# Recurrence of a bidirectional WKV kernel: when the result rows are turned on TensorE, and in which order its last two tiles are summed

## The chip, the cores and the metric

The kernel runs on one core of a Trainium2 chip. The metric is the device time of one execution in microseconds (us), and the median of the runs is compared. Before the change three runs took 1113.6, 1116.46 and 1119.26 us, so the median is 1116.46. A profile of one further execution (1116.4 us) shows where the time goes. A core has five engines that each work through their own instructions in order and wait for one another by semaphores: TensorE (PE, with its weight loads PEld), VectorE (DVE), ScalarE (ACT), GpSimd (POOL) and SyncE (SP), which here only starts transfers. All numbers are float32.

## The reference

Two stages are computed on `x` of shape 4 x 1024 x 1024. The first is a recurrence over time in both directions; its result is the input of the second, two blocks of attention over 16 slots. Cut to what matters:

```python
ek = exp(min(k, 30));  ekv = ek * v              # here k = v = fside, r = x
a_t = a_{t-1} * decay + ekv_t                    # forward; the same in reverse
b_t = b_{t-1} * decay + ek_t
num = nf + nb - ekv + exp(min(u + k, 30)) * v
den = df + db - ek  + exp(min(u + k, 30))
x1  = sigmoid(r) * num / max(den, 1e-8) * (0.8 + 0.2 * tf)
for _ in range(2):                               # slot attention
    logits = rms(x1) @ compete_w.T + compete_b   # 16 slots; the 4 best tokens of each
    ...                                          # write slots, attend to them
    x1 = rms(x1 + x_b)
out = x + x1
```

## The kernel before

The recurrence works on 32 tiles `i` of 128 channels x 1024 time steps (4 batches, 8 tiles of channels each), with time along the free dimension. All work is issued in an order written out by hand (`pin`); each engine runs its own part of it in that order, so an instruction that waits holds up everything behind it on its engine. Of tile `i`, in the loop from L525:

- DVE makes four scans of 1024 steps (L314): forward over `ek`, forward over `ekv`, reverse over each (`den`, `num`), and three other passes (L354, L358, and L413 for tile `i - 1`). The reverse scans start from an edge value that ACT makes (L326) once the forward scan has ended.
- ACT computes the exponentials (L286, L306), the logarithm and exponential that make a reciprocal of `den` (L391, L393, `quo`), the square of the result (L428), and copies out of PSUM.
- POOL multiplies and clamps (L296, L302, L375, L406, L407) and makes the product of tile `i - 1` (L425), which is the result and also the last reader of that tile's `both` buffer. There are two such buffers.
- PE sums the numerators into `num` (L364), contracts the result (`gate`) and its square (in `quo`, of which there are two buffers) into `raw` for the logits (L436), and transposes the result into rows (`turn_half`, L450). These go through one PSUM bank, `ptr`, which a copy on ACT (L451) empties into `stage` before the next transposes; then ACT's queue sends `stage` to the rows in DRAM (L459). The same bank serves `projection`, 25 pieces of work on later weights (L481 to L506) that are strewn over the tiles.

Every fourth tile (`i % HK == 0`, HK is 4) ACT also computes the sigmoid of the next four tiles of `x` at once: a table load, one instruction over 128 x 4096, and a table load back (L273, L171). It stands between the two edges, in the place called `between`. `x` is loaded in groups of four tiles (`load_gates`), of which three are held. The rows of tile `i - 2` are turned in tile `i`, half by half, each half followed by its contraction of the square.

After the loop, from L592, the last tile is finished by halves: numerators, the rest of `raw`, then norms and logits of 1024 tokens x 16 slots x 4 batches. The transposes of tile 30's rows stand ahead of the last numerators, those of tile 31's rows after the logits. In `write_slots` the four best tokens of each slot are found and gathered from the rows in DRAM (L746); the gather waits until the last rows have landed.

Of the kernel before, what the change touches and what calls it, by code (L numbers as in the profile page):

```python
# [10 lines left out]
F32 = mybir.dt.float32  # L11
# [4 lines left out]
PSUM = bass.MemoryType.PSUM  # L16
DRAM = bass.MemoryType.DRAM

P = 128
# [19 lines left out]
def kernel(  # L39
# [71 lines left out]

    rc_stack = ExitStack()
    rc = rc_stack.enter_context(tc.tile_pool(name="rec_const", bufs=1))
    cond_sb = rc.tile([P, B, TD], F32, name="cond_sb")
# [3 lines left out]
    rec_stack = ExitStack()  # L118
    rec = rec_stack.enter_context(tc.tile_pool(name="rec", bufs=1))
    rec_ps = rec_stack.enter_context(tc.tile_pool(name="rec_ps", bufs=1, space=PSUM))  # L120

    def load(i):
        kf = rec.tile([P, L], F32, tag="kf", bufs=4, name=f"kf_{i}")
# [129 lines left out]
    with rec_stack:  # L253
# [176 lines left out]
        def contract(i, src, w, halves=(0, 1)):  # L430

            b, k = i // NK, i % NK
            rows_b = slice(32 * b, 32 * b + 32)
            for h in halves:
                pin(
                    nc.tensor.matmul(  # L436
                        raw[rows_b, ts(h, 512)],
                        lhs[:, w].rearrange("p h s -> p (h s)"),
                        src[:, ts(h, 512)],
                        start=(k == 0 and w == k),  # L440
                        stop=(k == NK - 1 and w == NK),
                    )
                )

        def turn_half(i, stage, h):

            xk = gate_of(i)
            ptr = rec_ps.tile([P, 4, P], F32, tag="ptr", bufs=1, name=f"ptr_{i}_{h}")
            for q in range(4):
                pin(nc.tensor.transpose(ptr[:, q, :], xk[:, ts(4 * h + q, P)], ident))  # L450
            pin(nc.scalar.copy(stage[:, 4 * h : 4 * h + 4, :], ptr))  # L451

        def staged(i):
            return rec.tile([P, NT, P], F32, tag="stage", bufs=1, name=f"stage_{i}")
# [67 lines left out]
        ek[0] = terms_exp(0, kf[0], halves)  # L522
        ek[1] = terms_exp(1, kf[1])
        ekv[0] = terms(0, kf[0], ek[0], halves)
        for i in range(N):  # L525
# [4 lines left out]
            both[i], edge[i] = sums_a(  # L530
                i,
                ek[i],
                ekv[i],
                [every] if past else halves,
                lambda: own_exp(i, kf[i], own[i]),
                lambda: gates(i // HK) if i % HK == 0 else None,
            )
            if i == 0:
                move(npost_col, npost.rearrange("(k p) -> p k", p=P))
                move(bo_col, bo.rearrange("(k p) -> p k", p=P))  # L540
            if i == 3:
                move(npost_bc, npost.partition_broadcast(P))
            if i % HK == 2 and i // HK + 2 < N // HK:
                load_gates(i // HK + 2)
            if 5 <= i < 9:
                wo_next.append(load_rows(wo, i - 5, f"wp{i - 5}"))
            if N // 2 - 2 <= i < N // 2 + 8 and i % 2 == 0:
                load_ahead(0, (i - N // 2 + 2) // 2)
            if i >= N - 2:
                for n in range(2):  # L550
                    load_ahead(0, 5 + 2 * (i - N + 2) + n)
            if older:
                stage = staged(i - 2)
                for h in range(2):
                    turn_half(i - 2, stage, h)
                    contract(i - 2, quo[i - 2], NK, (h,))
                send(i - 2, stage)
            for _ in range(min((0, 1, 2, 2)[i % HK], len(projection)) if i > HK * 2 else 0):
                projection.pop(0)()
            if past:  # L560
                gated(i - 1, both[i - 1], quo[i - 1])
            if i == HK:
                pin(
                    nc.gpsimd.tensor_tensor(
                        cw_next, cw_sb, npost_col.unsqueeze(2).to_broadcast([P, NK, S]), ALU.mult
                    )
                )
            if i + 1 < N:
                ekv[i + 1] = terms(i + 1, kf[i + 1], ek[i + 1])
            den_sum(both[i], own[i])  # L570
            floor(both[i])
            if past:
                newton(i - 1, both[i - 1], quo[i - 1], num_ps[i - 1])
                product(i - 1, both[i - 1][:, 0, :], nc.gpsimd)
                store_turned(i - 1)
            ov = own_value(i, kf[i], own[i])
            num_ps[i] = rec_ps.tile([P, L], F32, tag="num", bufs=1, name=f"num_{i}")
            add_negated(num_ps[i], ov, True)
            if i == N - 1:
                break  # L580
            numerator(i, both[i], edge[i])
            quo[i] = guess(i, both[i])
            if i + 2 < N:
                ek[i + 2] = terms_exp(i + 2, kf[i + 2])
            if past:
                square(i - 1, quo[i - 1])
# [11 lines left out]
        spread_cols = spread.rearrange("p b h s -> p (b h s)")  # L598
        quo[i] = guess(i, both[i], [part for _, part in halves])
        square(i - 1, quo[i - 1])  # L600
        stage = staged(i - 1)
        for h in range(2):
            turn_half(i - 1, stage, h)
        send(i - 1, stage)
        for h, part in halves:
            numerator_half(i, both[i], edge[i], h)
            gated(i, both[i], quo[i], part)
            add_negated(num_ps[i], both[i][:, 1, :], False, (h,))
        for h, part in halves:
            newton(i, both[i], quo[i], num_ps[i], part, num_ps[i])  # L610
            product(i, num_ps[i], nc.vector, part)
            square(i, quo[i], part)

        def spread_squares(h, part):
            pin(nc.vector.tensor_copy(raw_sb[:, part], raw[:, part]))
            pin(nc.tensor.matmul(sq[:, part], spread_cols, raw_sb[:, part], start=True, stop=True))

        for h, part in halves:
            contract(i - 1, gate_of(i - 1), NK - 2, (h,))
            if h == 0:  # L620
                spread_squares(*halves[0])
            contract(i - 1, quo[i - 1], NK, (h,))
            contract(i, gate_of(i), NK - 1, (h,))
            contract(i, quo[i], NK, (h,))
# [30 lines left out]
        norm_root(halves[1][1])  # L655
        norm_logits(halves[1][1])

        turned_last = rec_ps.tile([P, NT, P], F32, tag="num", bufs=1, name="turned_last")
        for t in range(NT):
            pin(nc.tensor.transpose(turned_last[:, t, :], gate_of(i)[:, ts(t, P)], ident))  # L660
        stage = rec.tile([P, 2, L], F32, tag="both", bufs=2, name="stage_last")[:, 0, :]
        stage = stage.rearrange("p (t c) -> p t c", c=P)
        for h in range(2):
            part = slice(4 * h, 4 * h + 4)
            pin(nc.scalar.copy(stage[:, part, :], turned_last[:, part, :]))
        send(i, stage)
    rc_stack.close()
    keep = ctx.enter_context(tc.tile_pool(name="keep", bufs=1))

# [651 lines left out]
```

## Time and profile before

| | us |
|---|---|
| median of three runs | 1116.46 (1113.6 to 1119.26) |
| the profiled execution | 1116.4 |
| its span, first to last instruction | 1114.6 |
| recurrence: last forward scan's tile starts | 410.49 |
| logits complete | 443.0 |
| the gather starts | 447.80 |
| attention, two blocks | the rest |

In the profile a line gives an instruction group as line, engine, operation and `out<-in`; a number with x is a count, and what stands in brackets is the time that the engine had been idle and what ended it. Each tile's start is taken where DVE's scan over `ek` starts. The granted clock is what TensorE was given: 1.00 is full speed, 0.50 half.

### The profile page before, as it was taken

The numbers are of one execution on the slowest core, as the hardware profiler recorded it, in microseconds if no ns is written. First come the engines' busy times: TensorE is split into PE (matmuls) and PEld (weight loads), VectorE is DVE, ScalarE is ACT, GpSimd is POOL, SyncE is SP. The second block draws the span as 40 slices with busy tenths as digits, with TensorE's granted clock in tenths as the row PEclk, the third lists the DMA queues.
The fourth block names the chain that finished last, engine by engine and source line by source line (L and its number), as shares of the span: only waits on it lengthen the run. The fifth ranks groups of instructions, "written<-read, shape, count | busy, mean of one in ns | idle before, by whom it ended". The sixth has DMA issues, their size and how long they took to land.

```text
span 1114.6 us, 11896 instructions
## 1 busy us (share of the span) xinstructions
PE 965.5 (87%) x4116; PEld 541.4 (49%) x4116; DVE 768.0 (69%) x1049; ACT 508.4 (46%) x791; POOL 546.4 (49%) x417
## 2 busy tenths in 40 slices
PE   1677787887878876799999999996899999999996
PEld 0222232322323322484666666664584767676764
DVE  7999999999999996133666666566233555555555
ACT  6475767667676744012343434444112333333332
POOL 5989898989989882200222222222100344444444
PEclk9889998989989889699999999999799999999999
DMA  8558563857644363491477777562671355555554
GB/s 267 188 152 278 155 210 108 269 153 241 211 149 134 111 217 105 166 399 61 166 264 260 259 278 279 193 223 90 230 298 57 133 208 189 207 190 207 190 204 155
DMA packets 121787, 218.78 MB, mean 196 GB/s; under 512 B 10928, under 2 KB 76592, under 8 KB 121728
## 3 DMA queue, kind: packets, MB, share of 16 engines
q1 hardware_dynamic: 87872, 199.15, 51.0%
q10 hardware_dynamic: 33280, 16.78, 5.4%
q0 software_dynamic: 576, 2.10, 0.6%
q8 instruction: 32, 0.52, 0.2%
q14 instruction: 27, 0.22, 0.1%
HBM read 150.90 MB, written 67.11 MB: 196 GB/s over the span
## 4 chain that ended last, share of the span: by engine, by line
PE 60%; DVE 17%; POOL 8%; ACT 7%; issue 5%; DMA 2%; SPq 1%; POOLq 0%; ACTq 0%; DVEq 0%
PE psc L1052 20%; PE po L1109 19%; DVE both L314 12%; PE pk L912 3%; PE pkv L842 3%; PE raw L436 2%; PE ptr L1040 2%; PE pv L980 2%; POOL gate L425 2%; PE pw L792 2%; PE num L364 2%; DVE both L413 2%; POOL gate L407 1%; POOL ekv L302 1%; DVE ov L358 1%
## 5 line engine op out<-in xcount | busy, mean ns | idle before, releaser
L1052 PE MATMUL psc<-km,xt 128*128 128x272 f32 (+1 forms) x1024 | 238.4, 386 | 0.0
L1109 PE MATMUL po<-vm,e 128*128 128x512 f32 x512 | 230.4, 593 | 0.9 <-ACT e L1099 0.9
L1052 PEld LDWEIGHTS psc<-km,xt 128*128 128x128 f32 x1024 | 189.5, 190 | 29.1
L1086 POOL TENSOR_TENSOR e<-e,den 128x256 f32<-128x256 f32 x64 | 40.6, 634 | 252.3 <-DVE den L1084 231.4
L314 DVE TENSOR_TENSOR_SCAN both<-columns,edges,both 128x1024 f32<-128x1024 f32 x64 | 148.3, 2317 | 3.1 <-ACT edges L326 3.1
L1109 PEld LDWEIGHTS po<-vm,e 128*128 128x128 f32 x512 | 94.8, 190 | 95.7 <-issue 85.4
L364 PE MATMUL num<-ov,minus_ident 128*128 128x512 f32 x128 | 84.6, 796 | 60.8 <-DVE ov L358 60.8
L1150 DVE SCALAR_TENSOR_TENSOR y<-y,inv,npost_bc 128x1024 f32<-128x1024 f32 x62 | 79.6, 1284 | 41.3 <-POOL inv L1145 41.3
L1118 DVE TENSOR_TENSOR y<-po,y 128x512 f32<-128x512 f32 x128 | 85.7, 674 | 30.9 <-PE po L1109 30.6
L1138 ACT ACTIVATE junk<-y 128x1024 f32<-128x1024 f32 x63 | 66.7, 1059 | 69.5 <-DVE y L1150 69.4
L406 POOL TENSOR_TENSOR both<-both,quo 128x1024 f32<-128x1024 f32 (+1 forms) x33 | 75.8, 2296 | 32.9 <-ACT quo L393 31.5
L1145 POOL TENSOR_TENSOR inv<-mean,minus_half 128x1 f32<-128x1 f32 x64 | 35.6, 557 | 96.7 <-DVE mean L1143 96.7
L364 PEld LDWEIGHTS num<-ov,minus_ident 128*128 128x128 f32 x128 | 27.8, 241 | 104.7 <-DVE ov L358 64.5
L314 DVE TENSOR_TENSOR_SCAN both<-columns,ek 128x1024 f32<-128x1024 f32 (+1 forms) x32 | 71.6, 2236 | 9.1 <-POOL gate L425 9.1
L302 POOL TENSOR_TENSOR ekv<-ek,kf 128x1024 f32<-128x1024 f32 (+1 forms) x33 | 75.7, 2294 | 2.6
L407 POOL TENSOR_TENSOR gate<-gate,quo 128x1024 f32<-128x1024 f32 (+1 forms) x33 | 75.4, 2286 | 0.0
L1099 ACT COPY e<-pet 128x256 f32<-128x256 f32 x64 | 23.8, 372 | 113.0 <-PE pet L1098 112.9
L1247 POOL TENSOR_TENSOR y<-y,xin 128x1024 f32<-128x1024 f32 x31 | 73.2, 2360 | 1.4 <-DVE y L1150 1.4
L425 POOL TENSOR_TENSOR gate<-gate,both 128x1024 f32<-128x1024 f32 x31 | 73.3, 2364 | 0.6
L436 PE MATMUL raw<-gate,lhs 128*32 128x512 f32 x128 | 65.2, 632 | 9.3 <-POOL gate L425 9.3
L436 PE MATMUL raw<-quo,lhs 128*32 128x512 f32 x128 | 71.5, 642 | 0.0
L314 DVE TENSOR_TENSOR_SCAN both<-columns,ekv 128x1024 f32<-128x1024 f32 (+1 forms) x32 | 71.3, 2230 | 0.0
(189 smaller groups left out, 1474.1 us busy)
## 6 DMA issues: line engine op xcount, KB each, us to landing
y<-rows SPq DMA_DIRECT2D x64, 512.0 KB, 4.3
kf<-in_ft_dram SPq DMA_DIRECT2D x32, 512.0 KB, 5.8
gate<-in_xt_dram SPq DMA_DIRECT2D x32, 512.0 KB, 6.8
turned_rows<-gate SPq DMA_DIRECT2D x32, 512.0 KB, 3.7
xt<-turned_rows SPq DMA_DIRECT2D x32, 512.0 KB, 5.4
rows<-y SPq DMA_DIRECT2D x32, 512.0 KB, 3.0
xin<-in_x_dram SPq DMA_DIRECT2D x32, 512.0 KB, 4.6
rows<-stage ACTq DMA_DIRECT2D x31, 512.0 KB, 3.3
```

Of the source, the lines that this page charges most:

```text
L302: pin(nc.gpsimd.tensor_tensor(ekv[:, part], ek[:, part], kf[:, part], ALU.mult))
L314: nc.vector.tensor_tensor_scan(dst[:, way], dec, src[:, way], start, ALU.mult, ALU.add)
L364: nc.tensor.matmul(num_ps[:, ts(h, 512)], minus_ident, src[:, ts(h, 512)], start=first, stop=not first,)
L406: pin(nc.gpsimd.tensor_tensor(den, den, quo[:, part], ALU.mult))
L407: pin(nc.gpsimd.tensor_tensor(xk, xk, quo[:, part], ALU.mult))
L425: pin(engine.tensor_tensor(xk, xk, factor[:, part], ALU.mult))
L436: nc.tensor.matmul(raw[rows_b, ts(h, 512)], lhs[:, w].rearrange("p h s -> p (h s)"), src[:, ts(h, 512)], start=(k == 0 and w == k), stop=( ...
L1052: nc.tensor.matmul(psc[g][:, :n], xt_g[g][:, k, :], maps["km"][:, g // NT, k, :n], start=(k == 0), stop=(k == NK - 1),)
L1109: nc.tensor.matmul(po, et[:, ts(c, P)], vm[:, c, ts(h, 512)], start=(c == 0), stop=(c == 1),)
L1118: pin(nc.vector.tensor_add(half, po, half))
L1150: pin(nc.vector.scalar_tensor_tensor(y[g], y[g], inv[g], npost_bc, ALU.mult, ALU.mult))
L1247: pin(nc.gpsimd.tensor_add(y[g - 1], y[g - 1], xin[g - 1]))
```

## The change

In tiles with a sigmoid no rows are turned. The rows that would have been due there (tile `4m - 2`) are transposed by halves at the ends of tiles `4m + 1` and `4m + 2`, and copied in the tile after, at `between`, from where the second copy also starts the send. They have a buffer of their own, `late_stage`, whose memory held `cond_sb` at the start. Since the group of `x` is read one tile longer, the loads of a later group are issued one tile later. The weights `wo` are loaded at tiles 2 to 5 instead of 5 to 8, and the pieces of `projection` start at tile 5 instead of 9, with 0, 1, 1, 2 of them by `i % 4` instead of 0, 1, 2, 2.

At the end the rows of tile 30 are no longer turned ahead of the last numerators. PE sums the numerators first, with contractions of tile 30 between and behind them, then those of tile 31; the rows of tiles 30 and 31 are turned after the logits' squares, into four PSUM banks, copied and sent one after the other.

```diff
+    cond_sb = rec.tile([P, L], F32, tag="late_stage", bufs=1, name="cond_sb")
+    cond_sb = cond_sb.rearrange("p (b n) -> p b n", n=TD)
...
-            pin(nc.scalar.copy(stage[:, 4 * h : 4 * h + 4, :], ptr))
+            return lambda stage: pin(nc.scalar.copy(stage[:, 4 * h : 4 * h + 4, :], ptr))
...
+            tag = "late_stage" if i % HK == 2 else "stage"
+            return rec.tile([P, NT, P], F32, tag=tag, bufs=1, name=f"stage_{i}")
...
-                lambda: gates(i // HK) if i % HK == 0 else None,
+                lambda: gates(i // HK) if i % HK == 0 else late_copy() if late_copy else None,
...
-            if i % HK == 2 and i // HK + 2 < N // HK:
+            if i % HK == 3 and i // HK + 2 < N // HK:
                 load_gates(i // HK + 2)
-            if 5 <= i < 9:
-                wo_next.append(load_rows(wo, i - 5, f"wp{i - 5}"))
+            if 2 <= i < 6:
+                wo_next.append(load_rows(wo, i - 2, f"wp{i - 2}"))
...
             if older:
+                now = i % HK > 0
                 stage = staged(i - 2)
                 for h in range(2):
-                    turn_half(i - 2, stage, h)
+                    if now:
+                        copy = turn_half(i - 2, h)
                     contract(i - 2, quo[i - 2], NK, (h,))
-                send(i - 2, stage)
-            for _ in range(min((0, 1, 2, 2)[i % HK], len(projection)) if i > HK * 2 else 0):
+                    if now:
+                        copy(stage)
+                if now:
+                    send(i - 2, stage)
+                else:
+                    late_stage = stage
+            for _ in range(min((0, 1, 1, 2)[i % HK], len(projection)) if i > HK else 0):
...
+            h = i % HK - 1
+            if i > HK and h in (0, 1):
+                j = i - i % HK - 2
+                copy = turn_half(j, h)
+
+                def late_copy(j=j, h=h, copy=copy, stage=late_stage):
+                    copy(stage)
+                    if h == 1:
+                        send(j, stage)
+
             add_negated(num_ps[i], both[i][:, 1, :], False)
...
-        stage = staged(i - 1)
-        for h in range(2):
-            turn_half(i - 1, stage, h)
-        send(i - 1, stage)
-        for h, part in halves:
+        for n, (h, part) in enumerate(halves):
             numerator_half(i, both[i], edge[i], h)
             gated(i, both[i], quo[i], part)
             add_negated(num_ps[i], both[i][:, 1, :], False, (h,))
+            if n == 0:
+                contract_half(i - 1, False, h)
+        contract_half(i - 1, True, 1)
+        for squares in (False, True):
+            contract_half(i - 1, squares, 0)
...
+        for squares in (False, True):
+            contract_half(i, squares, 1)
+        contract_half(i, False, 0)
+        spread_squares(*halves[0])
+        contract_half(i, True, 0)
...
+        for n in range(4):
+            for q in range(4):
+                block = gate_of(i - 1 + n // 2)[:, ts(4 * (n % 2) + q, P)]
+                pin(nc.tensor.transpose(banks[n][:, q, :], block, ident))
...
+        for j, stage in ((i - 1, staged(i - 1)), (i, stage_last)):
+            for h in range(2):
+                bank = banks[2 * (j - i + 1) + h]
+                pin(nc.scalar.copy(stage[:, 4 * h : 4 * h + 4, :], bank))
+            send(j, stage)
```

`contract_half(j, squares, h)` contracts half `h` of tile `j`'s squares or gate into `raw`; `halves` is the second half first.

More of the change, by code (lines that the diff above doesn't have):

```diff
@@ L113 @@
     rc = rc_stack.enter_context(tc.tile_pool(name="rec_const", bufs=1))
-    cond_sb = rc.tile([P, B, TD], F32, name="cond_sb")
+    rec_stack = ExitStack()
+    rec = rec_stack.enter_context(tc.tile_pool(name="rec", bufs=1))
+    rec_ps = rec_stack.enter_context(tc.tile_pool(name="rec_ps", bufs=1, space=PSUM))
+    cond_sb = rec.tile([P, L], F32, tag="late_stage", bufs=1, name="cond_sb")
+    cond_sb = cond_sb.rearrange("p (b n) -> p b n", n=TD)
     nc.sync.dma_start(cond_sb, cond.partition_broadcast(P))
@@ L117 @@
     nc.sync.dma_start(w_sb, w_decay)
-    rec_stack = ExitStack()
-    rec = rec_stack.enter_context(tc.tile_pool(name="rec", bufs=1))
-    rec_ps = rec_stack.enter_context(tc.tile_pool(name="rec_ps", bufs=1, space=PSUM))
     def load(i):
@@ L443, in contract, with turn_half @@
                 )
-        def turn_half(i, stage, h):
+        def turn_half(i, h):
             xk = gate_of(i)
@@ L450, in turn_half @@
                 pin(nc.tensor.transpose(ptr[:, q, :], xk[:, ts(4 * h + q, P)], ident))
-            pin(nc.scalar.copy(stage[:, 4 * h : 4 * h + 4, :], ptr))
+            return lambda stage: pin(nc.scalar.copy(stage[:, 4 * h : 4 * h + 4, :], ptr))
         def staged(i):
-            return rec.tile([P, NT, P], F32, tag="stage", bufs=1, name=f"stage_{i}")
+            tag = "late_stage" if i % HK == 2 else "stage"
+            return rec.tile([P, NT, P], F32, tag=tag, bufs=1, name=f"stage_{i}")
         def send(i, stage):
@@ L524 @@
         ekv[0] = terms(0, kf[0], ek[0], halves)
+        late_copy = None
         for i in range(N):
@@ L535 @@
                 lambda: own_exp(i, kf[i], own[i]),
-                lambda: gates(i // HK) if i % HK == 0 else None,
+                lambda: gates(i // HK) if i % HK == 0 else late_copy() if late_copy else None,
             )
+            late_copy = None
             if i == 0:
@@ L600, with contract_half @@
         square(i - 1, quo[i - 1])
-        stage = staged(i - 1)
-        for h in range(2):
-            turn_half(i - 1, stage, h)
-        send(i - 1, stage)
-        for h, part in halves:
+        def contract_half(j, squares, h):
+            contract(j, quo[j] if squares else gate_of(j), NK if squares else j % NK, (h,))
+        for n, (h, part) in enumerate(halves):
             numerator_half(i, both[i], edge[i], h)
@@ L616, in spread_squares @@
             pin(nc.tensor.matmul(sq[:, part], spread_cols, raw_sb[:, part], start=True, stop=True))
[L618 to L624, printed above, removed]
+        for squares in (False, True):
[3 more added lines that the diff above has]
+        contract_half(i, True, 0)
         store_turned(i)
@@ L656 @@
         norm_logits(halves[1][1])
[L658 to L666, printed above, removed]
+        banks = [rec_ps.tile([P, NT, P], F32, tag="num", bufs=1, name="turn")]
+        banks = [
+            rec_ps.tile([P, 4, P], F32, tag=tag, bufs=1, name=f"turn_{tag}")
+            for tag in ("ptr", "columns")
+        ] + [banks[0][:, :4, :], banks[0][:, 4:, :]]
+        for n in range(4):
+            for q in range(4):
+                block = gate_of(i - 1 + n // 2)[:, ts(4 * (n % 2) + q, P)]
+                pin(nc.tensor.transpose(banks[n][:, q, :], block, ident))
+        stage_last = rec.tile([P, 2, L], F32, tag="both", bufs=2, name="stage_last")[:, 0, :]
+        stage_last = stage_last.rearrange("p (t c) -> p t c", c=P)
+        for j, stage in ((i - 1, staged(i - 1)), (i, stage_last)):
[3 more added lines that the diff above has]
+            send(j, stage)
     rc_stack.close()
```

## The prediction

> **What bounds the kernel now.** I read the page first, then, for the recurrence (0 to 447 us), who waited for whom, VectorE's instructions in time, and stretches of single tiles. The page gives the whole: TensorE looks like the bound, but that is the attention; in the recurrence VectorE (DVE) is.
>
> ```profile
> PE 965.5 (87%) x4116; PEld 541.4 (49%) x4116; DVE 768.0 (69%) x1049; ACT 508.4 (46%) x791; POOL 546.4 (49%) x417
> ```
>
> By tile (us, then busy time of PE, weight loads, DVE, ACT, POOL, then granted clock): three tiles, and the tile after a sigmoid.
>
> ```profile
> 192.61:229.97 37.36, 29.55 (x96) 10.43 (x96) 37.25 (x22) 26.28 (x32) 34.57 (x18) 0.90 0.68 225
> 229.97:244.20 14.23, 12.75 (x33) 4.50 (x32) 12.59 (x8) 9.65 (x13) 11.46 (x6) 0.89 0.52 147
> ```
>
> DVE is full at 37.25 of 37.36, so a tile costs 12.44 us of DVE work. The starts of each tile's first scan give its period: 12.44 to 12.47 everywhere, but 14.04 at tile 1 and 14.24, 13.84, 15.24, 14.23, 12.97, 15.25, 13.53 at tiles 5, 9, 13, 17, 21, 25, 29. Over 12.44 those last seven lose 1.80, 1.40, 2.80, 1.79, 0.53, 2.81, 1.09 = 12.2 us. DVE's waits say for whom (total, times, longest):
>
> ```profile
> DVE both L314 <- POOL gate L425: 9.1, 8, 1.5
> DVE raw_sb L615 <- PE raw L436: 5.1, 2, 3.9
> DVE num L413 <- PE num L364: 3.3, 1, 3.3
> DVE both L314 <- ACT edges L326: 3.1, 4, 1.3
> ```
>
> Where POOL's lateness comes from stands in the sigmoid tile 16 (start 217.52), in time:
>
> ```profile
> 225.06 1.28 ACT L171 ACT_TABLE_LOAD   x1
> 225.66 1.04 POOL L375 TENSOR_SCALAR both<-both 128x1024 f32<-128x1024 f32 x1 [0.77 <-DVE both L354]
> 226.36 0.29 ACT L326 ACTIVATE edges<-both,turn 128x1 f32<-128x1 f32 x1
> 226.56 0.57 ACT L451 COPY stage<-ptr 128x512 f32<-128x512 f32 x1
> ...
> 227.18 1.12 PE L450 MATMUL ptr<-ident,gate 128*128 128x128 f32 x4 [2.99 <-ACT stage L451]
> ...
> 228.23 1.92 PE L436 MATMUL raw<-quo,lhs 128*32 128x512 f32 x2
> ...
> 230.24 1.06 ACT L391 ACTIVATE quo<-both 128x1024 f32<-128x1024 f32 x1 [1.32 <-PE raw L436]
> ```
>
> The second copy's bank `ptr` is free only once ACT, back from the sigmoid, has made the first copy; the second transposes and the contraction of `quo` queue behind; the logarithm, which overwrites that `quo` buffer, waits for it until 230.24. POOL waits for the quotient, and its product (L425) frees `both` late for tile 18's first scan.
>
> **Part 1: no rows turned beside sigmoids.** Both contractions of `quo` then run at about 222.7 to 224.7, right after the sums. What is late next is the floor (ends 226.70) and the edge (ends 226.65): the logarithm starts at 226.75, 3.5 us earlier. An undisturbed tile starts it 9.21 us after its first scan (214.29 in tile 15, start 205.08); 226.75 is 9.23. So POOL is back on schedule and the whole stall is gone: up to 12.2 us. Tile 1 keeps its 1.6: no rows are turned in tile 0.
>
> **Part 2: where the work goes.** A group's withheld rows are transposed at the ends of tiles 4m+1 and 4m+2, between the contraction of the gate and the sum of numerators (0.7 us of PE each), and copied in the tile after, between the two edges. The copies are 14 of 0.58 us, the same number as removed; there ACT waits for DVE anyway (33.0 us over 28 waits for edges), so they cost nothing; without that cover 0.6 us each. Projections stay 25 pieces, in a pattern 0,1,1,2 instead of 0,1,2,2.
>
> Steady at full clock, tile 4m+3 from its start: gate contraction to +1.7, late transposes +2.4, numerators +4.3, first transposes +4.8, first copy +4.85 (tile 15 had 4.7), then the ring transpose, copy, transpose, copy through the single bank (5.0 us for two halves and two projections, from 158.14 to 163.18 in tile 11) to +9.9. The logarithm waits 0.6 us over its 9.25. POOL has 0.6 us idle ahead of its floor and frees `both` 0.87 us before the scan asks (229.10 against 229.97): no stall.
>
> At half clock it is otherwise. With one projection less, PE in tile 4m+2 is idle from +7.95 until `ov` comes at +10.3: 2.35 us. What follows such gaps (PE busy in a window of 3.41 us, then the clock granted in the window and the next):
>
> ```profile
> 147.70:151.11 3.41, 1.47 (x18) 0.86 (x19) 3.41 (x4) 2.49 (x4) 3.41 (x3) 1.00 1.03 360
> 151.11:154.52 3.41, 3.41 (x5) 0.70 (x4) 3.41 (x2) 3.38 (x4) 3.34 (x3) 0.50 0.80 220
> 198.80:202.21 3.41, 2.01 (x10) 0.84 (x8) 3.38 (x4) 1.69 (x4) 3.41 (x3) 1.00 1.01 406
> 202.21:205.62 3.41, 2.66 (x6) 0.93 (x7) 3.41 (x3) 3.38 (x4) 3.26 (x2) 1.00 1.03 388
> ```
>
> 1.47 of 3.41 busy was followed by half clock, 2.01 was not. With 1.7 idle as the limit, a gap of 2.35 trips it for window starts from +6.24 to +8.6, 2.36 of 3.41, about 4 groups of 6. The Trainium skill, "TensorE: Matmul & The Clock Gate", section "HAM oscillation — how this bites in real kernels", asks only that idle gaps stay under about 3.4 us; by it a 2.35 us gap leaves the clock alone and the full 12.2 is won. I go by the row.
>
> A half window takes 3.41/2 = 1.7 us from PE, as tile 11 shows (first copy at +5.73 instead of 4.7, last copy end at +10.77). With the late transposes ahead, tile 4m+3's ring ends at +11.6: the logarithm is 2.3 late, ACT brings the next tile's own exponential to +4.65, the first edge to +4.95 (DVE wants it at +4.36: 0.6 lost), the sigmoid ends later, the second edge at +11.5 (wanted at +10.85: 0.65 lost). That is 1.25 us, 1.0 where one projection is the shorter product, 1.15 in the mean: stall = lateness less 1.05. Four groups: 4.6 us. Bounds: none of six, 0; all six, 6.9. The group before tile 5 has no late rows yet and keeps its gain. Recurrence: 12.2 - 4.6 = 7.6 us.
>
> **Part 3: queues.** The four gate loads go one tile later and wait on SP for PE's transposes at +2.4; the keys' load stands ahead of them, weights behind. Needed five tiles (62 us) on, landing in 6.8: nothing. The `wo` loads come three tiles earlier; tile 3 then issues about 5 MB (keys, four gates, `wo`, norm row, two stores). At 406 GB/s (the stretch 11.2 to 23.1) that is 12.9 us in a tile of 12.44; keys have 22 us of lead and land in 5 to 7: nothing, at worst about 1 us once. The buffer for `cond` moves, no instruction with it.
>
> **Part 4: the end.** The chain now:
>
> ```profile
> 423.43 0.57 ACT stage L451
> 424.00 0.04 issue
> 424.04 0.66 PE ptr L450 x4
> 424.70 1.72 PE num L364 x4
> 426.42 4.50 PE raw L436 x10
> ...
> 431.68 1.12 PE sq L616 x2
> 432.81 2.71 PE raw L436 x6
> ```
>
> Without the two turned halves, PE goes from the sum over `ov` (ends 422.79) straight into numerators (1.9 for two halves), eight half contractions (0.9 each) and the spread (1.1): 422.8 + 1.9 + 7.2 + 1.1 = 433.0, where the chain has 435.52. The factors come in time: the product's second half is there at 427.8, first wanted at 430.1. Gain 2.5; the added late transposes make tile 31's logarithm 0.8 late (420.7), which POOL, busy to 422.13, hides; I take 2.4. Then 16 transposes (2 us) and four copies (0.58) with two sends follow the roots: the last send is 1.5 us later against the logits, and lands (3.2) at about 443.6, while the gather's token is ready at 446.97 - 2.5 = 444.5. Hidden by 0.9; beyond it, one for one. Bounds of the end: 0 to 2.5.
>
> **Sum.** 7.6 + 2.4 = 10.0 us. The profiled execution took 1116.4 (span 1114.6 and 1.8 around it): 1106.4, span 1104.6. The median of the runs is 1116.46, the same to 0.1: 1106.5.
>
> **Rivals.**
> A, the sum above: 1106.5, own range 1104 to 1109.
> B, the clock stays full: 12.2 + 2.4, so 1101.9. For it: the skill's rule, and tile 14's window at 2.01 busy. Against: four windows under 1.5 busy that fell (151, 216, 267, 305).
> C, the change doesn't do what it says: the stall only changes its owner, from the turned rows to the ring of five fillings in tile 4m+3 and the late sigmoid behind it, at 1.75 a group as now. Left are tile 5's 1.8 and the end's 2.4: 1112.3. For it: ACT's 43.5 us of waits for `ptr` show how tight the ring is.
> D, slower: half-clock windows follow each other in the ring, since PE is busy 0.66 us of each 1.35 there. Lateness is 0.6 + 1.7 a window, stall 1.05 less; six groups cancel the 14.6 us at a stall of 2.43, that is 1.7 windows a group. Two give 1119.6, three 6 x 4.65 - 14.6 = 13.3 slower: 1129.8. Two windows in a row do occur (175 to 182); but the ring in tile 14 kept its clock.
>
> **From cases to numbers.** A 0.50, B 0.22, C 0.19, D 0.09. A measurement here can tell about 0.5% (5.6 us) from no change: below 1110.9 is faster. A, B and 0.06 of C are faster: 0.78; the rest of C, 0.13, is the same; D 0.09 slower. The range 1101 to 1112.5 takes in B and most of C and leaves out D and the edges of B and C, under 2 in 10.
>
> **What would show it.** Right: no wait of the logarithm L391 for PE, periods of 12.4 at tiles 5, 9 and on apart from edge waits near 0.6 us in sigmoid tiles after a half-clock window; DVE's waits for L425 down from 9.1 to about 1.5; `raw` complete 2.5 us earlier against tile 31's start; the token later than the last landing. Wrong: new DVE waits for `num` or keys, half clock through whole tiles, a gather held by the last rows, or a lost period in tiles 4m+2 and 4m+3.

## The result, and the profile after

The changed kernel takes 1103.74 us (median of four runs, 1101.15 to 1107.2); the kernel before, run beside it, 1115.03 (1112.52 to 1119.26). The ratio is 0.9887 with a 95% interval from 0.9859 to 0.9915. The prediction was 1106.5, its range 1101 to 1112.5.

The page's busy times hardly change, since none of the kernel's work was taken away:

```profile
PE 961.6 (87%) x4116; PEld 538.3 (49%) x4116; DVE 767.3 (70%) x1049; ACT 508.8 (46%) x791; POOL 546.3 (50%) x417
```

The stretch view gives busy time of PE, weight loads, DVE, ACT and POOL, then granted clock, DMA share and GB/s. These are the changed kernel's tiles 14 to 16, and tile 17, the one after a sigmoid:

```profile
190.55:227.89 37.34, 30.84 (x97) 10.49 (x96) 37.24 (x22) 27.98 (x35) 34.55 (x19) 0.91 0.74 239
227.89:240.40 12.51, 11.00 (x30) 3.64 (x30) 12.41 (x9) 7.31 (x11) 11.40 (x7) 0.90 0.44 127
```

Tile 17 took 14.23 us and takes 12.51, and DVE is full in it. Four of DVE's waits in the recurrence (total, times, longest):

```profile
DVE raw_sb L643 <- PE raw L437: 4.2, 2, 2.2
DVE both L315 <- ACT edges L327: 2.8, 4, 1.0
DVE num L414 <- POOL both L407: 2.5, 1, 2.5
DVE both L315 <- POOL gate L426: 2.4, 2, 2.2
```

The wait for POOL's product (L426, L425 before) falls from 9.1 us in eight times to 2.4 in two, of which 2.2 is tile 1. The cause is visible in the sigmoid tile 16, which starts at 215.44 (instructions in time: start, duration):

```profile
222.99 1.28 ACT L172 ACT_TABLE_LOAD   x1
223.59 1.04 POOL L376 TENSOR_SCALAR both<-both 128x1024 f32<-128x1024 f32 x1 [0.78 <-DVE both L355]
224.28 0.29 ACT L327 ACTIVATE edges<-both,turn 128x1 f32<-128x1 f32 x1
224.66 1.06 ACT L392 ACTIVATE quo<-both 128x1024 f32<-128x1024 f32 x1
...
225.63 2.34 DVE L315 TENSOR_TENSOR_SCAN both<-columns,edges,both 128x1024 f32<-128x1024 f32 x1
```

No copy of rows stands behind the edge, and the logarithm L392 starts 9.22 us after the tile's first scan, where it started 12.72 after it (230.24 - 217.52). 9.23 was predicted.

From tile 2's first scan to tile 31's the recurrence takes 364.92 us; it took 373.33. The periods are 12.44 to 12.52 but for tiles 8 (13.86), 12 (14.25) and 30 (12.75). What is left in tile 8 is the edges' two waits:

```profile
117.59 2.35 DVE L315 TENSOR_TENSOR_SCAN both<-columns,edges,both 128x1024 f32<-128x1024 f32 x1 [0.62 <-ACT edges L327]
124.13 2.35 DVE L315 TENSOR_TENSOR_SCAN both<-columns,edges,both 128x1024 f32<-128x1024 f32 x1 [0.60 <-ACT edges L327]
```

They follow two windows of half clock in a row, which begin at the end of tile 6. The stretch view, cut at the steps of the granted clock:

```profile
93.96:97.37 3.41, 1.25 (x6) 0.42 (x4) 3.38 (x4) 1.41 (x3) 2.71 (x3) 1.00 0.54 154
97.37:100.78 3.41, 2.81 (x4) 1.18 (x4) 3.41 (x3) 3.38 (x4) 3.40 (x2) 0.50 0.19 52
100.78:104.20 3.42, 3.42 (x5) 0.54 (x4) 3.42 (x2) 1.60 (x3) 3.42 (x3) 0.50 0.90 255
104.20:107.61 3.41, 3.41 (x15) 1.70 (x14) 3.38 (x3) 0.90 (x3) 3.14 (x2) 1.00 0.36 84
```

PE, idle 2.75 us ahead of the own values, is busy for only 1.25 of the first window; the next two are granted 0.50 and reach 4.1 us into tile 7 (start 100.09). Tile 7's logarithm then starts at 112.11, 12.02 after its first scan and not 9.21.

The end, as the chain of work in order of time (start, duration):

```profile
413.04 2.84 PE num L365 x6
415.88 0.98 PE raw L437 x2
416.86 1.05 PE num L365 x2
417.91 5.28 PE raw L437 x12
...
423.22 0.70 DVE raw_sb L643
423.92 0.04 issue
423.96 1.12 PE sq L644 x2
425.09 0.99 PE raw L437 x2
```

`raw` is complete at 426.08, 23.39 us after tile 31's first scan at 402.69; it was 25.03 after it. The gather starts 35.71 after that scan; it started 37.31 after it. The gain of the end is 1.60, not 2.4.

### The profile page after: what moved, and what is told of

The parts are those of the page before. It is cut to its first block, busy times and chain, and to the rows that moved or that the text cites. A ratio compares the mean times of both kernels' runs of the same rounds, so it can differ in the third digit from the quotient of the medians.

```text
span 1101.9 us, 11887 instructions
## 1 busy us (share of the span) xinstructions
PE 961.6 (87%) x4116; PEld 538.3 (49%) x4116; DVE 767.3 (70%) x1049; ACT 508.8 (46%) x791; POOL 546.3 (50%) x417
## 4 chain that ended last, share of the span: by engine, by line
PE 60%; DVE 24%; issue 5%; ACT 4%; POOL 3%; DMA 3%; SPq 1%; POOLq 0%; DVEq 0%; ACTq 0%
PE psc L1085 20%; PE po L1142 19%; DVE both L315 17%; DVE both L414 3%; PE pk L945 3%; PE pkv L875 3%; PE raw L437 2%; PE ptr L1073 2%; DVE ov L359 2%; PE pv L1013 2%; PE num L365 2%; PE pw L825 1%; PE pet L1131 1%; PE pmix L807 1%; PE poc L1158 1%
## 5 line engine op out<-in xcount | busy, mean ns | idle before, releaser
L365 PE MATMUL num<-ov,minus_ident 128*128 128x512 f32 x128 | 87.6, 821 | 96.1 <-DVE ov L359 96.1
L426 POOL TENSOR_TENSOR gate<-gate,both 128x1024 f32<-128x1024 f32 x31 | 73.3, 2363 | 1.2
L437 PE MATMUL raw<-gate,lhs 128*32 128x512 f32 x128 | 71.2, 681 | 0.6 <-POOL gate L426 0.6
L1176 DVE TENSOR_SCALAR mean<-total 128x1 f32<-128x1 f32 x64 | 9.9, 154 | 85.4 <-ACT junk L1171 46.0
```

What stands on the lines that cost most here:

```text
L365: nc.tensor.matmul(num_ps[:, ts(h, 512)], minus_ident, src[:, ts(h, 512)], start=first, stop=not first,)
L426: pin(engine.tensor_tensor(xk, xk, factor[:, part], ALU.mult))
L437: nc.tensor.matmul(raw[rows_b, ts(h, 512)], lhs[:, w].rearrange("p h s -> p (h s)"), src[:, ts(h, 512)], start=(k == 0 and w == k), stop=( ...
```

## The experiments

Three stretches separate the parts of the change in any profile: **the loop**, from tile 2's first scan to tile 31's; **the end**, from there to the issue of the gather; and **the rest**, from the mixing of the gathered rows to the last instruction, in which the kernels do the same work. A window means one of 3.41 us that is granted half clock. The fourth column counts, for the new loop, how many of the six groups have a window across the start of tile 4m + 3 (m from 1 to 6); the sixth says if one lies over tile 31's sum of own values. A tile's stall is what its period has over 12.44 us.

| kernel | loop, end | loop us | groups | end us | window | rest us | median us (runs) |
|---|---|---|---|---|---|---|---|
| before | old, old | 373.33 | | 37.31 | no | 661.5 | 1115.03 (4) |
| before_again | old, old | 373.26 | | 37.19 | no | 659.9 | 1114.6 (1) |
| end_only | old, new | 371.87 | | 35.74 | no | 664.6 | 1116.41 (12) |
| end_again | old, new | 373.50 | | 35.73 | no | 661.9 | 1115.29 (1) |
| changed | new, new | 364.92 | 4 | 35.71 | no | 658.2 | 1103.74 (4) |
| after_again | new, new | 362.59 | 4 | 37.38 | yes | 666.5 | 1104.4 (7) |
| loop_only | new, old | 362.35 | 2 | 37.21 | no | 663.3 | 1106.55 (4) |
| loop_again | new, old | 362.34 | 4 | 38.75 | yes | 663.0 | 1108.47 (1) |
| filler | new, filled | 361.30 | 0 | 37.37 | yes | 662.0 | 1108.19 (4) |
| gap_turn | new, moved | 361.50 | 2 | 37.34 | yes | 662.1 | 1105.96 (4) |
| gap_wide | new, 0,2,0,2 | 362.66 | 4 | 37.30 | yes | 661.6 | 1107.9 (10) |
| split_raw | new, split | 361.87 | 3 | 36.31 | yes | 661.6 | 1104.62 (6) |
| best | 0,1,2,2, split | 362.27 | 2 | 34.83 | no | 662.3 | 1105.75 (6) |
| warm | filled, split and filled | 361.99 | 0 | 34.86 | no | 664.0 | 1105.15 (6) |

Beside loop_only, end_only, filler and gap_turn the kernel before took 1115.15 us in the median of 15 runs; beside after_again, gap_wide, split_raw and best 1115.98 (15); beside warm and the three single runs 1115.91 (11). So kernels of different groups are compared by their ratios to it.

**One part alone.** loop_only has the late rows and the old end:

```diff
-        for n, (h, part) in enumerate(halves):
+        stage = staged(i - 1)
+        for h in range(2):
+            turn_half(i - 1, h)(stage)
+        send(i - 1, stage)
+        for h, part in halves:
...
-        banks = [rec_ps.tile([P, NT, P], F32, tag="num", bufs=1, name="turn")]
+        turned_last = rec_ps.tile([P, NT, P], F32, tag="num", bufs=1, name="turned_last")
```

> The late rows, the later gate loads and the new pattern of projections alone; the end of the recurrence as before (tile 30's rows turned ahead of the last numerators). Two stretches are read: M, from the first scan of tile 2 to that of tile 31 (before 373.3 us, changed 364.9), and E, from there to the first matmul of the gathered rows (before 42.7, changed 41.1). If the two parts are independent: M about 365, E about 42.7, 8.4 us faster than before. If the end's order is what pays, M stays near 373 or E near 41.

Measured: 1106.55, ratio 0.9925 (0.9908 to 0.9942). The loop takes 362.35 us, which is 11.0 less than before and 2.6 less than was expected. Tile 4m + 1 never stalls.

end_only has the old loop and the new end:

```diff
             if older:
-                now = i % HK > 0
                 stage = staged(i - 2)
                 for h in range(2):
...
+                    turn_half(i - 2, stage, h)
                     contract(i - 2, quo[i - 2], NK, (h,))
...
+                send(i - 2, stage)
```

> The new end alone, the loop as before. Independent parts: M 373.3, E 41.1, 1.6 us faster than before, too little for the runs to tell. If the loop's part hides something at the end (ACT free of copies), E differs by more than 0.5 from 41.1.

Measured: 1116.41, ratio 1.0012 (0.9995 to 1.0029). In the profile the gather starts 35.74 us after tile 31's first scan, 1.57 earlier than before; but its data came later (7.3 us from the gather to the first matmul of the mixing, 5.35 before), and the rest took 3.1 us more. Nor does the median show any gain: the interval leaves out one of 1.5 us. Why is not settled by these runs. Beside the new loop the medians neither show the end's gain nor exclude it: loop_only gains 8.6 us, the changed kernel 11.3 (and 11.6, below), with intervals that overlap.

**Is it the clock?** filler keeps PE busy in the gap of tile 4m + 2:

```diff
+            if i > HK and i % HK == 2:
+                keep_busy = rec_ps.tile([P, 4, P], F32, tag="ptr", bufs=1, name=f"busy_{i}")
+                for q in range(10):
+                    pin(nc.tensor.transpose(keep_busy[:, q % 4, :], ident, ident))
```

> The changed kernel with ten idle transposes of the identity in tiles 4m+2, behind the last projection, so that PE has no gap ahead of the next sums. If the stalls left in tiles 8 and 12 (1.42 and 1.81 us) come from the clock that falls in that gap: full clock at the change of those tiles, no stall over 0.5 in any sigmoid tile, M about 361.8, 3 us less. If they come from the five fillings of the single bank in tile 4m+3: they stay, M 364.9 or more, since a filling was added.

Measured: no window in that place in any of six groups, no tile from 2 to 30 over 12.51 us, and 361.30 us for the 29 of them: the floor. The stretches at the end of filler's tile 6:

```profile
93.20:96.60 3.40, 2.73 (x16) 1.49 (x14) 3.37 (x4) 1.16 (x3) 3.40 (x3) 1.00 0.55 154
96.60:100.00 3.40, 3.06 (x8) 1.03 (x8) 3.40 (x3) 3.37 (x4) 3.32 (x2) 1.00 0.06 16
```

The median did not follow (1108.19, ratio 0.9937, 0.9921 to 0.9954): in the profile a window over tile 31's sums cost the end 1.65.

gap_turn moves the late transposes into the gap, ahead of the own values' sum:

```diff
+            h = i % HK - 1
+            if i > HK and h in (0, 1):
+                j = i - i % HK - 2
+                copy = turn_half(j, h)
...
             ov = own_value(i, kf[i], own[i])
```

> The changed kernel with the late transposes moved ahead of the sums over ov in tiles 4m+1 and 4m+2, where PE idles, instead of behind the gate's contraction. By the clock: the gap shrinks from 2.35 to about 1.6 us and the busy stretch behind it by 0.7, so at least 0.7 less stall in each of tiles 8 and 12: M 361.7 to 363.5. By the count of fillings: nothing changes, M 364.9. If the transposes there hold up the sums instead, M is over 365.

Measured: 1105.96, ratio 0.992 (0.9898 to 0.9942), loop 361.50. Windows still cross the start of tiles 11 and 23, but with less work behind them cost 0.13 and 0.09. Two of six groups have one, so the move does not keep the clock up; it makes a window cheaper.

**The same kernels again.** after_again is the changed kernel, with no edit.

> The changed kernel itself, once more, beside the variants. Two theories of why its recurrence loses 3.5 us of the 12.2. Clock: the stalls of 1.42 and 1.81 us (tiles 8 and 12) belong to the position of the half-clock windows against the tiles, which differs in each execution; then the stalls fall on other tiles here or on none, tile 2's first scan to tile 31's takes 361.3 to 366 us, and each stalled tile has two half-clock windows in a row across the end of tile 4m+2. Ring: the five fillings of the bank in tile 4m+3 are too long as such; then tiles 8 and 12 are late again by 1.4 and 1.8 us, and the stretch takes 364.9. Time: 1103.7, 1101 to 1107, by both.

Measured: 1104.4, ratio 0.9903 (0.9877 to 0.9929). Tiles 8 and 12 now lose 0.00 and 0.48, tiles 16, 24 and 28 lose 0.17, 0.47 and 0.17. So the ring theory, by which tiles 8 and 12 are late as such, is wrong. The clock theory missed in one point: it asked for two windows in a row before each stall, and one was enough. In tile 11 (start 149.63) one window lies across the start:

```profile
140.87:144.28 3.41, 3.41 (x28) 1.47 (x27) 3.38 (x3) 1.35 (x3) 3.33 (x3) 1.00 0.03 10
144.28:147.69 3.41, 0.51 (x12) 0.24 (x3) 3.41 (x4) 1.53 (x3) 2.73 (x3) 1.00 0.55 154
147.69:151.10 3.41, 3.41 (x5) 0.88 (x5) 3.41 (x2) 3.41 (x4) 3.40 (x3) 0.50 0.41 116
151.10:154.51 3.41, 3.41 (x12) 1.40 (x12) 3.41 (x3) 1.41 (x3) 3.41 (x3) 1.00 0.64 192
```

Three instructions of the same stretch, from the timeline: the sum that the window slows (1.98 at full clock), the late logarithm, the one edge that DVE waits for.

```profile
147.51 3.64 PE L365 MATMUL num<-ov,minus_ident 128*128 128x512 f32 x4 [2.90 <-DVE ov L359]
...
160.70 1.06 ACT L392 ACTIVATE quo<-both 128x1024 f32<-128x1024 f32 x1
...
172.72 2.35 DVE L315 TENSOR_TENSOR_SCAN both<-columns,edges,both 128x1024 f32<-128x1024 f32 x1 [0.39 <-ACT edges L327]
```

The logarithm is 11.07 after the first scan, 1.86 late, for a stall of 0.48. In the changed kernel's first profile it was 2.81 and 3.20 late (tiles 7 and 11) for stalls of 1.42 and 1.81. All three say: stall = lateness less 1.4. It holds throughout: of the 23 tiles 4m + 4 in the 14 profiles that lose over 0.1 us, each loses 1.38 or 1.39 less than the logarithm before it was late.

loop_again is loop_only, with no edit of its own.

> The loop of the changed kernel with the old end, profiled once more, for the same question: the gather 37.2 us after tile 31's first scan without a half-clock window 10 to 14 us after that scan, about 38.9 with one; by the rival 37.2 in either case. Recurrence 361.3 to 365 us, stalls only in tiles 4m+4 with a half-clock window across the start of tile 4m+3.

Measured: loop 362.34, stalls of 0.29, 0.16, 0.41 and 0.17 in tiles 12, 16, 24 and 28, each behind a window across the start of the tile before. The five profiles with the changed loop unaltered (changed, after_again, loop_only, loop_again, split_raw) have 30 groups. In 13 no window crosses the start of tile 4m + 3, and none of these stalls by over 0.03; nor does any of the 12 of filler and warm. In 15 a single window does, for 0.21 in the mean (0.00 to 0.48); in two a double, for 1.42 and 1.81. The old end does lose to a window over tile 31's sum of own values: here it is 38.75, against 37.21 without.

before_again is the kernel before, with no edit.

> The kernel before, profiled once more. Question: does the old end also lose 1.7 us when a half-clock window falls over the own values' sum of tile 31? If so, the new end is worth 1.6 us at equal position of the windows. The gather comes 37.3 us after tile 31's first scan without a window between 10 and 14 us after that scan, and about 39 with one; by the rival, that the old end has no such gap, it is 37.3 wherever the windows lie. The recurrence: 371.5 to 373.5 us from tile 2's first scan to tile 31's.

Measured: 1114.6, loop 373.26, end 37.19 with no window over the sum. This profile alone couldn't answer the question; loop_again did.

end_again is end_only, with no edit of its own.

> The old loop with the new end, profiled once more: the gather 35.7 us after tile 31's first scan without a half-clock window 10 to 14 us after that scan, 37.35 with one. Recurrence 371.5 to 373.5 us.

Measured: 1115.29, loop 373.50, end 35.73 with no window over the sum. So the new end is worth 1.5 us without a window there (37.24 less 35.73, means of three profiles each) and 1.4 with one (38.75 less 37.35, the mean of four).

**A wider gap.** gap_wide takes the projection out of tile 4m + 2:

```diff
-            for _ in range(min((0, 1, 1, 2)[i % HK], len(projection)) if i > HK else 0):
+            for _ in range(min((0, 2, 0, 2)[i % HK], len(projection)) if i > HK else 0):
```

> The changed kernel with the projections' pieces in the pattern 0,2,0,2 in place of 0,1,1,2: the piece of tile 4m+2 goes to tile 4m+1, so that TensorE's gap before the own values in tile 4m+2 grows from 2.35 to 3.5 us, and tile 4m+3 with its five fillings stays as it is. Clock: each of the six groups now has half-clock windows at the end of tile 4m+2, three or more of them stall by 0.6 to 1.8 us in tile 4m+4, so tile 2's first scan to tile 31's takes 366 to 370 us and the time is 2 to 5 us above the changed kernel: 1106 to 1109. Ring: tile 4m+3 is unchanged, so nothing moves: 362 to 365 us, 1103.7.

Measured: loop 362.66, stalls of 0.52, 0.18, 0.52 and 0.16, as in after_again, whose windows happened to lie in the same places. By the numbers the clock theory's forecast of 366 to 370 failed. The edit hadn't made its premise true: the gap ahead of tile 6's own values grew from 2.75 to 3.06 us, not by 1.15, since the turned halves before it come later too. It therefore says little of wide gaps. The median of 1107.9 (ratio 0.9938, 0.9918 to 0.9959) is 3.5 above after_again's; the profile doesn't show where, and that stays open.

**The accumulator in two.** split_raw gives each half of `raw` a tile of its own:

```diff
-        raw = rec_ps.tile([P, L], F32, name="raw")
+        raw = [rec_ps.tile([P, 512], F32, name=f"raw{h}") for h in range(2)]
...
-            pin(nc.vector.tensor_copy(raw_sb[:, part], raw[:, part]))
+            pin(nc.vector.tensor_copy(raw_sb[:, part], raw[h]))
```

> The changed kernel with the accumulator of the contractions as two tiles of 512 columns in place of one of 1024. Theory of the end: VectorE's copy of the second half's squares waits for a contraction of the first half, only because both halves are one tile, 0.86 us after its own last contraction; with two tiles the gather is issued 34.9 us after tile 31's first scan in place of 35.7, if no half-clock window lies over the sums there (with one, 1.7 later in both). Rival: TensorE is the bound of this chain throughout and the wait lies beside it; then 35.7 stays. Time: 0.8 us less than the changed kernel, 1102.9, or the same 1103.7; no more than the traces can tell apart.

Measured: the end takes 36.31 us with a window over the sum, where after_again's, with the same window, takes 37.38: 1.07 less. DVE's copies in split_raw:

```profile
420.75 0.69 DVE L643 COPY raw_sb<-raw 128x512 f32<-128x512 f32 x1 [1.12 <-PE raw L437]
423.64 0.69 DVE L643 COPY raw_sb<-raw 128x512 f32<-128x512 f32 x1 [2.20 <-PE raw L437]
```

and in after_again:

```profile
422.29 0.69 DVE L643 COPY raw_sb<-raw 128x512 f32<-128x512 f32 x1 [1.98 <-PE raw L437]
425.18 0.69 DVE L643 COPY raw_sb<-raw 128x512 f32<-128x512 f32 x1 [2.19 <-PE raw L437]
```

The first copy's wait falls by 0.86, one half contraction. The windows of the two profiles lie 0.5 us apart against tile 31's start, so the other 0.2 need not be the edit's. The median shows nothing of it: 1104.62, ratio 0.9905 (0.9878 to 0.9931).

**Both points, and the gaps filled.** best is split_raw with the old pattern of pieces; warm is split_raw with filler's transposes and sixteen more in tile 31:

```diff
+            for _ in range(min((0, 1, 2, 2)[i % HK], len(projection)) if i > HK * 2 else 0):
```

```diff
+            if i > HK and i % HK == 2 or i == N - 1:
+                keep_busy = rec_ps.tile([P, 4, P], F32, tag="ptr", bufs=1, name=f"busy_{i}")
+                for q in range(16 if i == N - 1 else 10):
+                    pin(nc.tensor.transpose(keep_busy[:, q % 4, :], ident, ident))
```

> Both points at once: pieces in the pattern 0,1,2,2 as in the kernel before, starting from tile 9, so that TensorE's gap in tile 4m+2 shrinks from 2.35 to 1.2 us; and the accumulator as two tiles. Clock: no half-clock windows at the ends of tiles 4m+2, tile 2's first scan to tile 31's in 361.3 to 362.5 us, the gather 34.9 after tile 31's first scan; time 1100 to 1103. Ring: tile 4m+3 has the same five fillings, so 364.9 stays, and the time is 1102.9 by the accumulator alone.

Measured: 1105.75, ratio 0.9908 (0.988 to 0.9937); loop 362.27, end 34.83. Windows still cross the starts of tiles 7 and 27, for 0.01 and 0.98. In tile 6 no piece stands in the gap yet, since they start at tile 9. In tile 26 the gap is 1.42 us, but PE also waited 0.68 ahead of the second piece, and was busy for 1.31 us of the window before: one more projection makes windows rarer and doesn't remove them. The longer work behind makes the one at tile 27 dear (2.36 late).

> The changed kernel with the accumulator as two tiles, ten idle transposes in TensorE's gap in tiles 4m+2, and sixteen (2.1 us) in its gap of 3.3 us in tile 31, which stands before the own values' sum. Clock theory: no window with TensorE under 1.6 us busy at either place, so no half-clock window across the start of a tile 4m+3 and none over tile 31's sums; tile 2's first scan to tile 31's takes 361.3 to 361.6 us, and the gather is issued 34.9 us after tile 31's first scan, not 36.3. Rival: the 1.65 us that the end lost in four of the six profiles of it are not the clock's but a matter of data arriving; then 36.3. Time: 1101 to 1104; the second block's own half-clock windows, 658 to 667 us from the mixing of slots to the end, stay as they are.

Measured: 1105.15, ratio 0.9897 (0.9872 to 0.9921). There is no window across the start of any tile 4m + 3 and none over tile 31's sums, and the end is 34.86, as the clock theory had it. With best's 34.83 that is 0.88 below the new end's 35.73 without a window, which is what the accumulator in two is worth. The loop is 361.99, not 361.6: tile 30 loses 0.68, behind a double window across the start of tile 29, a place that nothing was put into. Windows at tile 31's gap in after_again (gap, then sums at half clock):

```profile
403.67:407.08 3.41, 3.40 (x13) 1.05 (x11) 3.38 (x3) 1.35 (x3) 0.43 (x1) 1.00 0.98 333
407.08:410.50 3.42, 0.09 (x1) 0.09 (x1) 3.42 (x4) 1.17 (x2) 2.17 (x2) 1.00 1.05 356
410.50:413.91 3.41, 3.41 (x4) 1.36 (x5) 2.33 (x2) 2.37 (x4) 3.41 (x3) 0.50 0.81 238
```

The own values' sum in warm, from the timeline:

```profile
406.43 1.97 PE L576 MATMUL busy<-ident 128*128 128x128 f32 x16
409.64 1.98 PE L365 MATMUL num<-ov,minus_ident 128*128 128x512 f32 x4 [1.25 <-DVE ov L359]
```

and in loop_again:

```profile
410.10 3.54 PE L365 MATMUL num<-ov,minus_ident 128*128 128x512 f32 x4 [3.34 <-DVE ov L359]
```

With the gap filled the sum takes 1.98 us, without 3.54. No version beats the changed kernel: the intervals of best, warm and split_raw all overlap its own. The parts of 1 to 3 us that they do gain in the loop and the end are smaller than what the rest varies by (658.2 to 666.5).

## Why the prediction was right or wrong

**Part 1, the stall beside sigmoids: right, with one part of its cause unseen.** The logarithm starts where it was put (9.22 against 9.23), ACT's wait for `raw` is gone, and no tile 4m + 1 of any profile with the new loop stalls. The old loop's mean over four profiles is 372.99 us; the floor that filler reached is 361.30. So 11.7 was there to be had, where the forecast took 12.2 from its one profile.

The forecast put the old stall down to ACT's stay at the sigmoid alone. But in its lines of tile 16 the second transposes and contractions (1.12 and 1.92 us) ran at half clock. Tile 20 of the same profile has no window there, after the same wait for ACT:

```profile
278.77 0.66 PE L450 MATMUL ptr<-ident,gate 128*128 128x128 f32 x4 [2.94 <-ACT stage L451]
279.35 1.04 PE L436 MATMUL raw<-quo,lhs 128*32 128x512 f32 x2
...
280.55 1.06 ACT L391 ACTIVATE quo<-both 128x1024 f32<-128x1024 f32 x1 [0.50 <-PE raw L436]
```

Tile 21 then loses 0.53 us, where tile 17 lost 1.79. Of the 28 tiles 4m + 1 in the four profiles of the old loop, the seven without a window over that work lose 0.50 to 0.53, the 21 with one 1.09 to 2.81. So at full clock the order of work cost about 3.6 us (seven times 0.52); the rest of the 11.6 that these tiles lose in the mean goes with half clock, after PE had stood idle for 3 us and more. The change removes both at once, since no rows are turned there any more.

**Part 2, what the half clock gives back: right in mechanism and place, too large in size.** The forecast had a window in about four of six groups; the changed kernel had four, after_again four, and the five profiles of this loop 17 of 30. That count is in part luck: the gap is 2.75 us in tile 6, not 2.35, which by the forecast's limit of 1.7 us idle makes nearly five of six; but that limit is too low, since of the windows with 1.5 to 1.75 us of work only one in four was followed by half clock (below). Its price failed: "stall = lateness less 1.05", 1.0 to 1.25 a group. The slack is 1.4, and a single window makes the logarithm at most 1.86 late, as in tile 11, not 2.3: the forecast had added 0.6 of lateness, but with the clock up (warm) the logarithm starts 9.21 to 9.46 after the first scan. A single window costs 0.21, a double 1.4 to 1.8. The loss in the first profile is 3.5 (tiles 8, 12 and 30), in the others 0.5 to 1.3, not 4.6. The gain of the loop is 8.4 in the profiled pair and 10.2 in the mean (372.99 less 362.81), not 7.6.

The rule of the Trainium skill ("TensorE: Matmul & The Clock Gate", section "HAM oscillation — how this bites in real kernels") that was set against the row, gaps under about 3.4 us leave the clock alone, does not hold here: a gap of 2.75 us was enough. To go by the row was right for the mechanism; that the rule's sum for the loop, 12.2, lies nearer to the gain of most profiles is because a window costs so little.

**Part 3, queues: right as far as seen.** No DVE wait for keys, gates or `num` in tiles 2 to 30 came up.

**Part 4, the end: right in sign, too large in size.** 1.5 at like position of the windows, not 2.4. The step that was off is "eight half contractions (0.9 each) and the spread": it took PE to run them without a break. The copy of the second half of `raw`, one tile with the first, waits for one half contraction more than it needs, and PE then waits for the copy: 0.86, which split_raw took back (0.88 in best and warm). The last rows were to land 0.9 before the token is ready and did so by 0.55 (436.96 against 437.51).

What the forecast didn't see: with the new loop, a window lay over tile 31's own values in six of the nine profiles that leave its gap empty, and in none of four with the old. Where it does, the end loses what it gained (37.38 against the old kernel's 37.31). The 1.6 of the profiled pair is thus the better case, and the end gives about 0.7 in the mean of the two profiles of the changed kernel.

**The sum.** 7.6 + 2.4 was forecast; the means give 10.2 and 0.7, 10.9, and the medians 11.3 and 11.6. That the total came within 3 us is in part luck: one term was too small and the other too large. Of the profiled pair's 12.7 us (1114.6 less 1101.9), 8.4 is the loop, 1.6 the end, 0.6 was lost ahead of tile 2, and 3.3 is the rest, which the change does not touch: the half-clock windows at the second block's slots were 17 us long before and 10 after.

**Rivals.** B had the mechanism wrong (windows do fall) and the number nearly right. C: the ring of five fillings costs nothing without a window. D: no profile has more than two windows in a row there, and two only in 2 of 30 groups.

## What to carry to other kernels

Where PE is not the bound, what counts of its clock is when windows of reduced clock lie on work that others wait for: price a window as its lateness less the slack of what waits, both read at the consumer, and expect that the next execution has it elsewhere. Look for the gain of an edit in its own stretch of several profiles, since a stretch that the edit doesn't touch can vary by more than the edit is worth. And if one half of a buffer that is declared as one tile is read while the other is still written, look for a wait between them (0.86 us here), which a sum of PE's work alone doesn't show.

## What the runs showed of the hardware that was not expected

**The clock follows the work in the window before.** Over all 14 profiles, cut into windows of 3.41 us at the steps of the granted clock (from 35 us on, without the last 12 us): of the windows at full clock in which PE was busy for under 1.5 us, 206 of 211 were followed by half clock; of those with 1.5 to 1.75 us, 10 of 39; of those with more, 24 of 3643. Of the windows at half clock, all 132 with under 2.75 us busy were followed by another, 24 of 44 with 2.75 to 3.0, and 24 of 251 with more. At half speed 2.95 us is the work of 1.5 at full: these counts fit one limit for both, some 45% of a window in work done. It explains the double window at tile 7 (2.81 busy at half clock was too little) and that a gap of 2.75 us or more may or may not trip it: in after_again tile 6's gap fell on two windows, busy for 1.85 and 2.22 us, and left the clock alone. Most exceptions recur at a few places. All 24 at half clock with over 3.0 us busy are in the mixing of slots; those at full clock with over 1.75 are in tiles 27 to 30, near 500 us and near the second block's slots. Why was not tried. That the work decides is shown by filler and warm: transposes put into the gap left none of 12 groups with a window, against 17 of 30.

**The windows' grid is not tied to the program.** Two executions of one kernel have it in different places, so that the changed kernel's loop lost 3.5 us in one and 1.3 in the other. In the rest the total of half clock at the second block's slots goes with its time: 10 us of it, 658.2; 14 us, 659.9; 17 us, 661.5 to 663.0 in eight profiles; 20 us, 663.3 and 664.0; 24 us, 664.6; 27 us, 666.5. So a spread of 8 us between executions goes with this one place; that the windows there cause it was not tried.

**The gather's time varies.** From its issue to the first matmul on its rows it took 4.65 to 7.31 us in the same work.
